# Performer attention of a 16-layer network: feature matmuls by row groups, head sums by column groups, one batch in two slots

## The chip, the cores and the metric

The kernel runs on one core of one Trainium2 chip, in one launch. The metric is the time of one execution in device microseconds. Before the change the median of three runs was 4373.4 us (4373.02 to 4376.56).

## The reference

The reference is a network of 16 layers on an array of 16 batches, 256 tokens and 128 channels. Each layer adds its result to x after a norm over the channels. The change touches one of them, the attention of `_L0_attn_b_ref` (a "performer"): 16 heads of 8 channels, 32 random features per head. Cut to that:

```python
def _phi(u, omega):                                  # u: b h s k (k=8), omega: m k (m=32)
    proj = jnp.einsum('bhsk,mk->bhsm', u, omega)
    sq = 0.5 * jnp.sum(u * u, axis=-1, keepdims=True)
    stab = jnp.max(proj, axis=-1, keepdims=True)
    return jnp.exp(proj - sq - stab) / jnp.sqrt(m) + 1e-06

q, k, v = (jnp.einsum('bsd,dhk->bhsk', x, w) for w in (wq, wk, wv))
pq, pk = _phi(q * scale, omega), _phi(k * scale, omega)
kv  = jnp.einsum('bhsm,bhsk->bhmk', pk, v)           # sums over the 256 tokens of a batch
z   = jnp.sum(pk, axis=2)
num = jnp.einsum('bhsm,bhmk->bhsk', pq, kv)
den = jnp.einsum('bhsm,bhm->bhs', pq, z)
out = (num / den[..., None]) ... @ wo
```

After it come a residual, a layer norm (`ln1`), a feed-forward part and a second layer norm.

## The kernel before

All activations stay on the chip as tiles of 128 channels (partitions) by 4096 tokens. Work goes by chunks of 512 tokens (8 of them, index `c`; a chunk is two batches), batches of 256 tokens (16, index `b`) and tiles of 128 tokens (32, index `n`). All matmuls are fp32.

`performer_attend` is written as steps. `tiles_in_slots` runs over slots `k` from -6 to 45 and in each slot goes down the list `steps`: an entry `(slot, every, many, what)` calls `what(n)` in slot `slot + n * every`. This is the program's order on every engine: each engine takes its instructions in this order, and a waiting one holds up those behind it. Four slots are one chunk. A PSUM bank is asked for with `self.bank()`; before the change all steps share eight banks, in turn.

The steps that matter, by name:

- `project(c)`: two matmuls (`wq`, `wk`) over a chunk; ScalarE copies each to `q` (scaled), GpSimd squares it to `sq`.
- `lengths(c)`: eight matmuls of `sq` against `w["half"]` give half the squared length of each head's vector; VectorE copies them to `nrm`. `values(c)`: four matmuls with `wv`, copied to `v` by ScalarE with a column of ones per group of four heads.
- `features(n)`: for one tile, the query side and the key side each take one matmul of 128 rows against the block-diagonal `w["om"]` (512 columns: 16 heads of 32 features). VectorE takes the maximum over each head's 32 features from PSUM (`tensor_reduce` into `sub`, L2298), adds `nrm`, and subtracts from PSUM into `f`; ScalarE takes the exponential of the 1024 columns, GpSimd scales and adds 1e-6 (L2304).
- `sums(b)`: eight matmuls (L504, 33 columns) of the key features against the values; VectorE masks them into `kv`. `turn(n)`: four transposes of the query features, copied to `ft` by ScalarE.
- `heads(n)`: four matmuls of `ft` against `kv` (36 columns: 32 sums and 4 denominators) give tokens by channels; VectorE takes the reciprocal of the denominators (L2340) and multiplies into `o`. `join(c)`: four transposes bring `o` back to channels by tokens, copied to `ot`.
- `out(c)`: one matmul with `wo`, and VectorE adds `h0` into `hb`. `end(0..2)`: the layer norm: a matmul that centres `hb`, a ScalarE copy, the square `nsq` on GpSimd, a matmul for the variance, Ln and Exp on ScalarE (`nrs`), a product on VectorE (L543) and a bias on ScalarE. `norm(0..2)`: the norm before the attention, for the last three chunks only; the other five were normed in the layer before.

The order within a slot before the change, from the list:

```python
(13, 4, NCH, end(2)), (12, 4, NCH, end(1)), (11, 4, NCH, end(0)), (10, 4, NCH, out), (9, 4, NCH, join),
(4, 1, NTILE, heads), (3, 2, B, sums), (2, 1, NTILE, turn), (0, 1, NTILE, features),
(-1, 4, NCH, lengths), (-1, 4, NCH, values), (-2, 4, NCH, project),
(-3, 4, NCH, norm(2)), (-5, 4, NCH, norm(1)), (-6, 4, NCH, norm(0)),
```

L504 is the helper `mm` (matmul), L508 `tr` (transpose), L528 `act` (ScalarE), L531 `tt` (VectorE), L534 `gt` (GpSimd). In the trace each fp32 matmul leaves two records.

Of the kernel before, what the change touches and what calls it, by code (L numbers as in the profile page):

```python
# [1649 lines left out]
class Fast(Net):  # L1650
# [598 lines left out]
    def performer_attend(self, w):  # L2249


        nc = self.nc
        h0, y = self.ha, self.hb
        s8 = 8.0**-0.25
        with ExitStack() as st:
            p = self.stage(st, "f2", 1)
            qk, nrm, vs, fs, kvs, fts, os, ots, ends = {}, {}, {}, {}, {}, {}, {}, {}, {}

            def project(c):
                s = self.chunk(c)  # L2260
                for side, wn in enumerate(("wq", "wk")):
                    pq = self.bank()
                    self.mm(pq, w[wn], h0[:, s])
                    q = p.tile([P, CH], F32, tag=f"q{side}", name="q", bufs=2)
                    self.act(q, pq, AF.Copy, scale=s8)
                    sq = p.tile([P, CH], F32, tag=f"sq{side}", name="sq", bufs=1)
                    self.gt(sq, q, q, ALU.mult)
                    qk[c, side] = q, sq

            def lengths(c):  # L2270
                pn = self.bank()
                for side in range(2):
                    for t in range(4):
                        at = (2 * t + side) * 16
                        self.mm(pn[:, at : at + 16], qk[c, side][1][:, t * P : t * P + P], w["half"])
                nrm[c] = p.tile([P, 4, 2, 16], F32, tag="nrm", name="nrm", bufs=2)
                nc.vector.tensor_copy(nrm[c].rearrange("p t s h -> p (t s h)"), pn[:, :P])
# [10 lines left out]
            def features(n):  # L2288
                c, t = divmod(n, 4)
                f = p.tile([P, 2, 16, 32], F32, tag="f", name="f", bufs=6)  # L2290
                sub = p.tile([P, 2, 16], F32, tag="sub", name="sub", bufs=2)
                pps = []
                for side in range(2):
                    pp = self.bank()
                    self.mm(pp, qk[c, side][0][:, t * P : t * P + P], w["om"])
                    pps.append(pp.rearrange("p (h m) -> p h m", h=16))
                for side in range(2):
                    nc.vector.tensor_reduce(sub[:, side], pps[side], AX.X, ALU.max)  # L2298
                self.tt(sub, sub, nrm[c][:, t], ALU.add)
                for side in range(2):  # L2300
                    self.tt(f[:, side], pps[side], sub[:, side, :, None].broadcast_to([P, 16, 32]), ALU.subtract)
                flat = f.rearrange("p s h m -> p (s h m)")
                self.act(flat, flat, AF.Exp)
                nc.gpsimd.tensor_scalar(flat, flat, 32.0**-0.5, 1e-6, ALU.mult, ALU.add)  # L2304
                fs[n] = f.rearrange("p s h m -> p s (h m)")

            def sums(b):
                pkv = self.bank()
                for g in range(4):
                    for u in range(2):  # L2310
                        n = 2 * b + u
                        self.mm(
                            pkv[:, g * 33 : g * 33 + 33], fs[n][:, 1, g * P : g * P + P], vs[n // 4][:, n % 4, g],
                            start=u == 0, stop=u == 1,
                        )
                kv = p.tile([P, 4, 36], F32, tag="kv", name="kv", bufs=2)
                pk3 = pkv[:, : 4 * 33].rearrange("p (g k) -> p g k", g=4)
                self.tt(kv[:, :, :32], pk3[:, :, :32], w["own"][:, None, :].broadcast_to([P, 4, 32]), ALU.mult)
                self.tt(
                    kv[:, :, 32:], pk3[:, :, 32:33].broadcast_to([P, 4, 4]),  # L2320
                    w["own1"][:, None, :].broadcast_to([P, 4, 4]), ALU.mult,
                )
                kvs[b] = kv

            def turn(n):
                pf = self.bank()
                for g in range(4):
                    self.tr(pf[:, g * P : g * P + P], fs[n][:, 0, g * P : g * P + P])
                ft = p.tile([P, 4, P], F32, tag="ft", name="ft", bufs=3)
                self.act(ft.rearrange("p g t -> p (g t)"), pf, AF.Copy)  # L2330
                fts[n] = ft

            def heads(n):
                ft, kv = fts.pop(n), kvs[n // 2]
                pn = self.bank()
                for g in range(4):
                    self.mm(pn[:, g * 36 : g * 36 + 36], ft[:, g], kv[:, g])
                pn3 = pn[:, :144].rearrange("p (g k) -> p g k", g=4)
                rd = p.tile([P, 4, 4], F32, tag="rd", name="rd", bufs=2)
                nc.vector.reciprocal(rd, pn3[:, :, 32:])  # L2340
                if n % 4 == 0:
                    os[n // 4] = p.tile([P, 4, P], F32, tag="o", name="o", bufs=2)
                self.tt(
                    os[n // 4][:, n % 4].rearrange("p (g h k) -> p g h k", g=4, h=4),
                    pn3[:, :, :32].rearrange("p g (h k) -> p g h k", h=4),
                    rd[:, :, :, None].broadcast_to([P, 4, 4, 8]), ALU.mult,
                )

            def join(c):
                pt = self.bank()  # L2350
                o = os.pop(c)
                for t in range(4):
                    self.tr(pt[:, t * P : t * P + P], o[:, t])
                ots[c] = p.tile([P, CH], F32, tag="ot", name="ot", bufs=1)
                self.act(ots[c], pt, AF.Copy)

            def out(c):
                s = self.chunk(c)
                ph = self.bank()
                self.mm(ph, w["wo"], ots.pop(c))  # L2360
                self.tt(y[:, s], h0[:, s], ph, ALU.add)

            def end(i):
                def step(c):
                    if i == 0:
                        s = y[:, self.chunk(c)]
                        ends[c] = self.norm_steps(p, s, s, "ps", w["ln1_g"], w["ln1_b"], "eps6")
                    ends[c][i]()

                return step  # L2370

            norm = lambda i: lambda c: self.norm_x_step(p, c, i)
            steps = [
                (13, 4, NCH, end(2)), (12, 4, NCH, end(1)), (11, 4, NCH, end(0)), (10, 4, NCH, out), (9, 4, NCH, join),
                (4, 1, NTILE, heads), (3, 2, B, sums), (2, 1, NTILE, turn), (0, 1, NTILE, features),
                (-1, 4, NCH, lengths), (-1, 4, NCH, values), (-2, 4, NCH, project),
                (-3, 4, NCH, norm(2)), (-5, 4, NCH, norm(1)), (-6, 4, NCH, norm(0)),
            ]
            self.tiles_in_slots(-6, NTILE + 14, steps)

    def performer_ffn(self, w):
        x, h0, y = self.x, self.ha, self.hb
# [1425 lines left out]
```

## Time and profile before

| | |
|---|---|
| median of the runs | 4373.4 us |
| profiled execution: time, span | 4392.96 us, 4391.2 us |
| share of the span busy: PE, PEld, VectorE, ScalarE, GpSimd | 90%, 50%, 59%, 54%, 48% |
| mean granted TensorE clock | 0.952 |
| attention stage, 870.3 to 1086.3 us | PE busy 205.15, VectorE 127.52, ScalarE 90.60, GpSimd 63.54 of 216.00; granted clock 0.94 |

The stage is about a twentieth of the span. It begins with the first matmul of `project` and ends with the last bias of the layer norm. Busy times are those of one profiled execution; PE's is the time in which matmuls are in the array, whatever the number of their columns.

### The profile page before, as it was taken

The page shows a single profiled execution, that of the slowest core. Times are in us where ns is not written, and L with a number is a line of the kernel's source. Part 1 is how long each engine was busy: PE and PEld are TensorE (multiplying, and loading weights), DVE is VectorE, ACT ScalarE, POOL GpSimd, SP SyncE. Part 2 cuts the span into 40 slices and gives each one's busy share as a digit, 9 for nine tenths or more (in the row PEclk, how much of TensorE's full clock was granted, in tenths as well). Part 3 has the DMA queues.
Part 4 walks back from the last instruction along what each step waited for, and adds up shares of the span by engine and source line. Part 5 has one row for each costly group of instructions (what it writes and reads, how often), then busy time and mean ns, then how long its engine had stood idle before and what let it go on. Part 6 is the DMA issues. An engine that isn't in the chain of part 4 may idle for free. (4 is left out here: it accounts for less than half of the span.)

```text
span 4391.2 us, 72802 instructions
## 1 busy us (share of the span) xinstructions
PE 3966.2 (90%) x28390; PEld 2202.4 (50%) x28390; DVE 2605.3 (59%) x4455; ACT 2376.1 (54%) x4549; POOL 2119.4 (48%) x1776
## 2 busy tenths in 40 slices
PE   7899999999899999995989969887999899899978
PEld 3455455466355445543975549643333344355333
DVE  4764566364366377456336643564888788386374
ACT  6665466444766456553447634445555554675442
POOL 4653355232455255315433334466998789521251
PEclk8999999999999999997999979998999999999989
DMA  1800000000000000001940029200000000000000
GB/s 59 332 1 1 11 1 1 19 1 1 19 1 1 1 3 1 1 0 49 310 162 10 15 88 326 86 18 16 1 1 1 3 1 1 15 2 18 6 0 20
DMA packets 78400, 176.36 MB, mean 40 GB/s; under 512 B 12606, under 2 KB 39108, under 8 KB 77920
## 3 DMA queue, kind: packets, MB, share of 16 engines
q1 hardware_dynamic: 65568, 148.40, 9.8%
q0 software_dynamic: 9120, 18.51, 1.2%
q8 instruction: 227, 3.72, 0.4%
q10 hardware_dynamic: 3360, 4.72, 0.3%
q14 instruction: 125, 1.02, 0.1%
HBM read 118.28 MB, written 54.20 MB: 39 GB/s over the span
## 5 line engine op out<-in xcount | busy, mean ns | idle before, releaser
L528 ACT ACTIVATE pt<-ps 128x512 f32<-128x512 f32 (+1 forms) x896 | 423.1, 537 | 408.1 <-PE ps L504 406.8
L504 PE MATMUL ps<-hb,w 128*128 128x512 f32 (+1 forms) x960 | 468.9, 623 | 5.4 <-issue 3.3
L531 DVE TENSOR_TENSOR t<-ps,tab 128x512 f32<-128x512 f32 x512 | 319.3, 683 | 196.1 <-ACT sq L528 191.3
L504 PE MATMUL ps<-w,hb 128*128 128x512 f32 (+2 forms) x896 | 415.1, 576 | 13.6 <-DVE t L531 11.3
L534 POOL TENSOR_TENSOR t<-t,ss 128x1024 f32<-128x1024 f32 x128 | 243.7, 1904 | 306.8 <-ACT ss L528 197.7
L534 POOL TENSOR_TENSOR t<-t,t 128x512 f32<-128x512 f32 x256 | 320.5, 1275 | 13.2 <-PE ps L504 10.1
L504 PEld LDWEIGHTS ps<-hb,w 128*128 128x128 f32 (+1 forms) x960 | 183.6, 196 | 273.5 <-issue 247.3
L531 DVE TENSOR_TENSOR u<-u,ps 128x384 f32<-128x384 f32 (+1 forms) x206 | 121.8, 595 | 277.8 <-ACT u L528 131.2
L534 POOL TENSOR_TENSOR nsq<-ha 128x512 f32<-128x512 f32 x112 | 123.2, 1100 | 314.1 <-ACT ha L528 297.3
L504 PE MATMUL ps<-nsq,ct 128*128 128x512 f32 x368 | 209.5, 654 | 53.9 <-POOL nsq L534 35.0
L528 ACT ACTIVATE pt<-pt 128x768 f32<-128x768 f32 (+1 forms) x160 | 169.5, 1060 | 154.6 <-DVE pt L531 154.6
L2199 POOL DMA_INDIRECT back<-y,x x142 | 139.1, 980 | 184.2 <-ACT y L528 90.2
L504 PE MATMUL ps<-qkt 64*128 64x192 f32 (+1 forms) x2048 | 216.2, 326 | 11.8 <-ACT pt L528 11.8
L504 PE MATMUL ps<-u,w 128*128 128x512 f32 (+1 forms) x448 | 218.8, 612 | 8.0 <-POOL u L534 8.0
L504 PE MATMUL ps<-ot,w 128*128 128x512 f32 x448 | 211.1, 604 | 15.2 <-POOL ot L534 6.9
L504 PE MATMUL ps<-xt,w 128*128 128x128 f32 x1704 | 219.8, 279 | 1.5 <-ACT xt L528 1.5
L504 PEld LDWEIGHTS ps<-qkt 64*128 64x128 f32 x2048 | 153.1, 188 | 133.3 <-ACT qkt L528 51.5
L504 PEld LDWEIGHTS ps<-w,hb 128*128 128x128 f32 x896 | 147.4, 192 | 139.4 <-issue 110.7
L531 DVE TENSOR_TENSOR pt<-ps,w 128x384 f32<-128x384 f32 (+1 forms) x320 | 171.2, 576 | 75.6 <-PE ps L504 72.2
L3705 POOL DMA_INDIRECT rows<-out,idx x128 | 126.4, 988 | 174.6 <-ACT out L528 125.6
L528 ACT ACTIVATE u<-ps,w 128x512 f32<-128x512 f32 x160 | 107.2, 685 | 186.3 <-PE ps L504 183.5
L531 DVE TENSOR_TENSOR pt<-pt,w 128x1024 f32<-128x1024 f32 (+1 forms) x96 | 181.1, 1886 | 42.3 <-ACT pt L528 42.3
(362 smaller groups left out, 9127.2 us busy)
## 6 DMA issues: line engine op xcount, KB each, us to landing
w<-in_moe_x SPq DMA_DIRECT2D x142, 533.0 KB
rows<-t SPq DMA_DIRECT2D x64, 520.0 KB
x<-rows SPq DMA_DIRECT2D x142, 65.0 KB
w<-in_local_f SPq DMA_DIRECT2D x8, 659.5 KB
y<-back ACTq DMA_DIRECT2D x16, 256.0 KB
y<-back SPq DMA_DIRECT2D x16, 256.0 KB
w<-in_local_f SPq DMA_DIRECT2D x4, 658.5 KB
back<-y,x POOLq DMA_INDIRECT x142
```

What stands on the lines that cost most here:

```text
L504: self.nc.tensor.matmul(out, lhsT, rhs, start=start, stop=stop)
L528: self.nc.scalar.activation(out, in_, func, **kw)
L531: self.nc.vector.tensor_tensor(out, a, b, op)
L534: self.nc.gpsimd.tensor_tensor(out, a, b, op)
L2199: nc.gpsimd.indirect_dma_start(views[i], bass.IndirectOffsetOnAxis(ap=x[:, C : C + 1].bitcast(I32), axis=0), y, None, bounds_check=2 * NT ...
L3705: nc.gpsimd.indirect_dma_start(views[(c * 2 + k) * 4 + t], bass.IndirectOffsetOnAxis(ap=idx[:, k, t : t + 1], axis=0), out[:, k, t], None,)
```

## The change

The change is confined to `performer_attend`.

- `features` works on a batch (two tiles, two sides) every second slot. Each of its 16 matmuls takes 32 rows (four heads) and 128 columns of `w["om"]`; the four row groups go to four PSUM banks. VectorE and ScalarE do the same work in two halves: two groups at a time are reduced, added, subtracted, exponentiated and scaled.
- PSUM is split: four banks (`f`) for `features`, four for all other steps.
- `kv` holds masked sums and masked denominators, 32 columns each. `heads` works on a batch: per group of four heads one matmul for the sums and one for the denominators, with `kv` as the 32 weight columns and `ft` as 256 moving columns, each group to its own 32 PSUM partitions. The result is channels by tokens. The division is Ln and Exp on ScalarE and a product on VectorE into `ot`.
- `join`, the reciprocal and `o` are gone. `lengths` writes in the order of the groups. The slots of `heads`, `sums` and `turn` move by one or two.

```diff
@@ lengths
+                by_group = pn[:, :P].rearrange("p (b g n h) -> p b g n h", b=2, g=4, h=4)
...
+                        self.mm(by_group[:, t // 2, :, t % 2 * 2 + side], qk[c, side][1][:, t * P : t * P + P], w["half"])
@@ features
-                f = p.tile([P, 2, 16, 32], F32, tag="f", name="f", bufs=6)
...
-                    self.mm(pp, qk[c, side][0][:, t * P : t * P + P], w["om"])
+                f = p.tile([P, 4, 2, 2, P], F32, tag="f", name="f", bufs=3)
+                sub = p.tile([P, 4, 16], F32, tag="sub", name="sub", bufs=2)
+                pps = [self.bank("f") for _ in range(4)]
+                for u in range(2):
+                    for side in range(2):
+                        for g in range(4):
+                            rows, t = slice(32 * g, 32 * g + 32), b % 2 * 2 + u
+                            self.mm(
+                                pps[g][:, (2 * u + side) * P : (2 * u + side) * P + P],
+                                qk[c, side][0][rows, t * P : t * P + P], w["om"][rows, g * P : g * P + P],
+                            )
+                for k in range(2):
+                    gs = slice(2 * k, 2 * k + 2)
+                    for g in (2 * k, 2 * k + 1):
+                        nc.vector.tensor_reduce(sub[:, g], pps[g].rearrange("p (n m) -> p n m", m=32), AX.X, ALU.max)
...
+                    self.act(flat, flat, AF.Exp)
+                    nc.gpsimd.tensor_scalar(flat, flat, 32.0**-0.5, 1e-6, ALU.mult, ALU.add)
@@ heads
+            def heads(b):
+                ft, kv = fts.pop(b), kvs.pop(b)
                 pn = self.bank()
-                for g in range(4):
-                    self.mm(pn[:, g * 36 : g * 36 + 36], ft[:, g], kv[:, g])
-                nc.vector.reciprocal(rd, pn3[:, :, 32:])
...
+                for k in range(2):
+                    for g in range(4):
+                        nc.tensor.matmul(pn[32 * g : 32 * g + 32, k * T : k * T + T], kv[:, k, g], ft[:, g], start=k == 0, stop=k == 1, skip_group_check=True)
+                rd = p.tile([P, T], F32, tag="rd", name="rd", bufs=2)
+                self.act(rd, pn[:, T:], AF.Ln)
+                self.act(rd, rd, AF.Exp, scale=-1.0)
...
+                self.tt(ots[b // 2][:, b % 2 * T : b % 2 * T + T], pn[:, :T], rd, ALU.mult)
-            def join(c):
...
@@ steps
-                (13, 4, NCH, end(2)), (12, 4, NCH, end(1)), (11, 4, NCH, end(0)), (10, 4, NCH, out), (9, 4, NCH, join),
-                (4, 1, NTILE, heads), (3, 2, B, sums), (2, 1, NTILE, turn), (0, 1, NTILE, features),
+                (13, 4, NCH, end(2)), (12, 4, NCH, end(1)), (11, 4, NCH, end(0)), (10, 4, NCH, out),
+                (6, 2, B, heads), (4, 2, B, sums), (3, 1, NTILE, turn), (0, 2, B, features),
                 (-1, 4, NCH, lengths), (-1, 4, NCH, values), (-2, 4, NCH, project),
...
-            self.tiles_in_slots(-6, NTILE + 14, steps)
+            with self.share(f=4, ps=4):
+                self.tiles_in_slots(-6, NTILE + 14, steps)
```

More of the change, by code (lines that the diff above doesn't have):

```diff
@@ L2256, in performer_attend @@
             p = self.stage(st, "f2", 1)
-            qk, nrm, vs, fs, kvs, fts, os, ots, ends = {}, {}, {}, {}, {}, {}, {}, {}, {}
+            qk, nrm, vs, fs, kvs, fts, ots, ends = {}, {}, {}, {}, {}, {}, {}, {}
             def project(c):
@@ L2271, in lengths @@
                 pn = self.bank()
+                by_group = pn[:, :P].rearrange("p (b g n h) -> p b g n h", b=2, g=4, h=4)
                 for side in range(2):
                     for t in range(4):
[L2274 to L2277, printed above, removed]
+                        self.mm(by_group[:, t // 2, :, t % 2 * 2 + side], qk[c, side][1][:, t * P : t * P + P], w["half"])
+                nrm[c] = p.tile([P, 2, 64], F32, tag="nrm", name="nrm", bufs=2)
+                nc.vector.tensor_copy(nrm[c].rearrange("p b n -> p (b n)"), pn[:, :P])
             def values(c):
@@ L2286, in values, with features @@
                 vs[c] = v
-            def features(n):
-                c, t = divmod(n, 4)
-                f = p.tile([P, 2, 16, 32], F32, tag="f", name="f", bufs=6)
[L2291 to L2294, printed above, removed]
-                    self.mm(pp, qk[c, side][0][:, t * P : t * P + P], w["om"])
[L2296 to L2305, printed above, removed]
+            def features(b):
+                c = b // 2
+                f = p.tile([P, 4, 2, 2, P], F32, tag="f", name="f", bufs=3)
[13 more added lines that the diff above has]
+                        nc.vector.tensor_reduce(sub[:, g], pps[g].rearrange("p (n m) -> p n m", m=32), AX.X, ALU.max)
+                    flat = sub[:, gs].rearrange("p g n -> p (g n)")
+                    self.tt(flat, flat, nrm[c][:, b % 2, 32 * k : 32 * k + 32], ALU.add)
+                    for g in (2 * k, 2 * k + 1):
+                        self.tt(
+                            f[:, g].rearrange("p u s (h m) -> p (u s h) m", h=4), pps[g].rearrange("p (n m) -> p n m", m=32),
+                            sub[:, g, :, None].broadcast_to([P, 16, 32]), ALU.subtract,
+                        )
+                    flat = f[:, gs].rearrange("p g u s m -> p (g u s m)")
+                    self.act(flat, flat, AF.Exp)
+                    nc.gpsimd.tensor_scalar(flat, flat, 32.0**-0.5, 1e-6, ALU.mult, ALU.add)
+                fs[b] = f
@@ L2310, in sums @@
                     for u in range(2):
-                        n = 2 * b + u
                         self.mm(
-                            pkv[:, g * 33 : g * 33 + 33], fs[n][:, 1, g * P : g * P + P], vs[n // 4][:, n % 4, g],
+                            pkv[:, g * 33 : g * 33 + 33], fs[b][:, g, u, 1], vs[b // 2][:, b % 2 * 2 + u, g],
                             start=u == 0, stop=u == 1,
                         )
-                kv = p.tile([P, 4, 36], F32, tag="kv", name="kv", bufs=2)
+                kv = p.tile([P, 2, 4, 32], F32, tag="kv", name="kv", bufs=2)
@@ L2317, in sums @@
                 pk3 = pkv[:, : 4 * 33].rearrange("p (g k) -> p g k", g=4)
[L2318 to L2322, printed above, removed]
+                own = w["own"][:, None, :].broadcast_to([P, 4, 32])
+                self.tt(kv[:, 0], pk3[:, :, :32], own, ALU.mult)
@@ L2323, in sums @@
+                self.tt(kv[:, 1], pk3[:, :, 32:33].broadcast_to([P, 4, 32]), own, ALU.mult)
                 kvs[b] = kv
             def turn(n):
+                b, u = divmod(n, 2)
+                if u == 0:
+                    fts[b] = p.tile([P, 4, T], F32, tag="ft", name="ft", bufs=2)
                 pf = self.bank()
                 for g in range(4):
-                    self.tr(pf[:, g * P : g * P + P], fs[n][:, 0, g * P : g * P + P])
-                ft = p.tile([P, 4, P], F32, tag="ft", name="ft", bufs=3)
@@ L2330, in turn @@
[L2330 to L2334, printed above, removed]
-                pn = self.bank()
-                for g in range(4):
-                    self.mm(pn[:, g * 36 : g * 36 + 36], ft[:, g], kv[:, g])
-                pn3 = pn[:, :144].rearrange("p (g k) -> p g k", g=4)
-                rd = p.tile([P, 4, 4], F32, tag="rd", name="rd", bufs=2)
-                nc.vector.reciprocal(rd, pn3[:, :, 32:])
[L2341 to L2347, printed above, removed]
@@ L2349, in join @@
-            def join(c):
[L2350 to L2355, printed above, removed]
+                    self.tr(pf[:, g * P : g * P + P], fs[b][:, g, u, 0])
+                self.act(fts[b][:, :, u * P : u * P + P], pf.rearrange("p (g t) -> p g t", g=4), AF.Copy)
+            def heads(b):
+                ft, kv = fts.pop(b), kvs.pop(b)
+                pn = self.bank()
+                for k in range(2):
[4 more added lines that the diff above has]
+                self.act(rd, rd, AF.Exp, scale=-1.0)
+                if b % 2 == 0:
+                    ots[b // 2] = p.tile([P, CH], F32, tag="ot", name="ot", bufs=2)
+                self.tt(ots[b // 2][:, b % 2 * T : b % 2 * T + T], pn[:, :T], rd, ALU.mult)
```

## The prediction

> **What bounds the kernel now.** The stage's busy times by stretches come first. The starts of the chunks' first feature matmuls (899.0, 919.2, 942.2, 966.9, 991.6, 1016.3, 1039.3 in the timeline) give the period: 24.7 us for a chunk in which the three norm steps also run, 23.0 without them, 20.2 at the start. Columns: length, then busy time (and instructions) of PE, PEld, DVE, ACT, POOL, granted clock, DMA.
>
> ```profile
> 966.90:991.60 24.70, 24.70 (x140) 17.48 (x139) 16.09 (x36) 12.12 (x20) 8.35 (x9) 1.00 0.00 1
> ...
> 1073.10:1076.60 3.50, 1.12 (x2) 0.30 (x2) 0.75 (x1) 1.41 (x3) 0.00 (x0) 0.99 0.00 0
> 1076.60:1080.00 3.40, 2.07 (x2) 0.50 (x2) 0.69 (x1) 0.54 (x1) 0.00 (x0) 0.50 0.00 0
> 1080.00:1083.40 3.40, 2.17 (x3) 1.14 (x4) 0.00 (x0) 0.12 (x2) 1.04 (x1) 0.50 0.00 0
> ```
>
> In a period TensorE has matmuls in the array all the time at clock 1.00; VectorE is 65% busy. TensorE bounds the stage. The last rows, the stage's end, show something else: where TensorE waits a large part of 3.4 us, the granted clock is 0.50 in the next stretch.
>
> The groups by shape, for 880 to 1080 us (last columns: busy, mean ns, idle before and what ended it):
>
> ```profile
> L504 PE MATMUL ps<-w,q 128*128 128x512 f32 x127 | 60.9, 604 | 0.0
> L504 PE MATMUL ps<-kv,ft 128*128 128x36 f32 x256 | 32.9, 276 | 0.0
> L504 PE MATMUL ps<-v,f 128*128 128x33 f32 x256 | 31.3, 277 | 0.6 <-POOL f L2304 0.6
> L528 ACT ACTIVATE f<-f 128x1024 f32<-128x1024 f32 x32 | 33.8, 1057 | 95.7 <-DVE f L531 95.7
> ```
>
> Records of 512 columns start 0.43 us apart, narrow ones about 0.1075, so a chunk takes: features 16 x 0.43 = 6.9, heads 32 x 0.1075 = 3.4, sums 3.4, turn 1.7, lengths 1.7, values 0.9, join 0.4, project 1.7, out 0.9, end 1.7, norm 1.7. The sum is 24.4 of the 24.7 measured.
>
> Last the timeline, for how long one link takes to hand over to the next. Columns: start, length.
>
> ```profile
> 980.81 1.06 ACT L528 ACTIVATE f<-f 128x1024 f32<-128x1024 f32 x1 [2.89 <-DVE f L531]
> 981.77 1.07 ACT L528 ACTIVATE q<-ps 128x512 f32<-128x512 f32 x2
> 981.95 1.05 POOL L2304 TENSOR_SCALAR f<-f 128x1024 f32<-128x1024 f32 x1 [3.38 <-ACT f L528]
> 983.07 2.04 POOL L534 TENSOR_TENSOR sq<-q 128x512 f32<-128x512 f32 x2
> 985.92 1.85 PE L504 MATMUL ps<-w,sq 128*128 128x16 f32 x16
> ...
> 1049.67 1.31 DVE L2298 TENSOR_REDUCE sub<-ps 128x16 f32<-128x512 f32 x2
> 1051.01 0.19 DVE L531 TENSOR_TENSOR sub<-sub,nrm 128x32 f32<-128x32 f32 x1
> 1051.24 1.29 DVE L531 TENSOR_TENSOR f<-ps,sub 128x512 f32<-128x512 f32 x2
> ```
>
> The first five lines are a chain: exponential, then the copies of q, which stand behind it on ScalarE, then the squares, which stand behind the scaling of f on GpSimd, then lengths. Today TensorE has other work meanwhile.
>
> **What TensorE saves.** Row and column groups run side by side elsewhere in this trace:
>
> ```profile
> 2513.92 1.14 PE L504 MATMUL ps<-qz,k 32*128 32x512 f32 x8
> 2514.99 0.66 PE L508 MATMUL ps<-ct,ha 128*128 128x128 f32 x4
> ...
> 3212.44 1.93 PE L3259 MATMUL ps<-pt,v 128*32 128x256 f32 x32
> 3214.19 0.61 PE L3259 MATMUL ps<-both,ct 128*32 128x256 f32 x8
> ```
>
> Eight records on four row groups take 1.07 us where eight in a row take 3.4; 32 records of 256 columns on four column groups take 1.75 us. So features(b), 32 records of 128 columns on four row groups, takes 8 x 0.1075 + 0.1 = 0.98 us, and heads(b), 16 records of 256 columns on four column groups, 0.98 us. Per chunk: minus 6.9, 3.4 and 0.4 (join), plus 4 x 0.98: TensorE's work falls from 24.4 to 17.6 us.
>
> **What the new order makes of it.** Per chunk VectorE's sum changes little: 16.1 us, minus four reciprocals (0.25) and four o products (0.29), plus two ot products (0.42 each, between the 0.29 of 128 columns and the 0.68 of 512; a 128x256 row has 0.424) and 2 x 0.13 for the wider denominators (128 columns at 0.29 for 16 at 0.16): 15.1. ScalarE's gets two Ln (0.39) and Exp (0.42), loses the ot copy (0.58): 13.2. No engine has 24 us of work, so if the stage keeps its length a chain does it. I follow the chains from the order of the instructions of the changed kernel, which the slot list fixes. Features now hold all four f banks until VectorE's last subtraction, so two batches of features never overlap.
>
> Chain A, from the first batch of a chunk to the second. VectorE's run for a batch: two times 2.86 us (1049.67 to 1052.53) = 5.7. Behind its last subtraction ScalarE has, in this order: the second exponential (0.1 until it starts, 0.96 until the next), the bias of end(2) (0.62 from start to start), the copy of turn (0.48), and only then Ln and Exp of heads (0.42, 0.42, from rows of another stage, 152.64 to 153.48). Then VectorE takes 0.1, ot 0.42, two kv products 0.58, and the next reductions. Sum: 9.8 us. TensorE needs 4.0 for turn, out, heads and sums; the second turn takes the bank that out's addition frees, which stands on VectorE behind the run, the L543 product and sometimes a norm product: about 7.5. So TensorE waits some 3.5 us, and its features are done at about 9.1, before ot.
>
> Chain B, from the second batch to the next chunk's first. Run 5.7, handover 0.1, second exponential 1.06, handover 0.1, scaling of f on GpSimd 1.05, two squares 2.04, handover 0.1: 10.2 us until lengths can finish, because project stands behind features in its slot and its q copies behind both exponentials. TensorE has project, norm(0), end(0) and a turn until then, 3.9 us, and then waits about 5.4. Behind it in TensorE's queue: the key half of lengths 0.86, values 0.86, norm(1) 0.86, end(1) 0.86, heads 0.98, sums 1.72, turn 0.43, features 0.98, and 0.2 until VectorE starts. Sum: 17.9.
>
> A + B = 27.7 us against 24.7 in the three chunks with norms, and 26.8 against 23.0 without. Over eight chunks: 3 x 3.0 + 5 x 3.8 = +28 us, with the clock at 1.00. I count the head and the tail as chunks.
>
> **The clock.** Before, it held 1.00 from 900 to 1060 us. Now each chunk has TensorE waits of about 3.5 and 5.4 us, longer than those that cost it the clock at the stage's end. The shortest half-clock stretch there is 3.4 us; in it TensorE does 1.7 us of work. On chain B 7.6 us of TensorE work follows the wait and all of it is on the path: one stretch costs 1.7 us, two cost 3.4. In chain A turn and features follow, 1.4 us with 0.7 of slack: up to 0.7. The bounds are 0 and 4.1 us a chunk, 0 and 33 us in all; I take 2.5 a chunk, +20, one stretch in B and the slack used up in A, as the nearest rows, the stage's end, show the loss in nearly every wait. The Trainium skill ("TensorE: Matmul & The Clock Gate", section "Why this matters for your kernels") says to leave no idle gap over about 3 us between bursts, since one idle window of about 3.4 us halves the clock. It speaks against this change; by it both waits lose the clock, and the sum has the upper bound.
>
> The same skill ("TensorEngine Tiling (Array Packing)", section "PSUM Bottleneck") warns that after tiling the copies out of PSUM may bound. By that alone the chunk would come to VectorE's 15 to 16 us, a gain; what I price is VectorE's and ScalarE's order, not their sums.
>
> **The sum.** +28 and +20 give +48 us: the profiled 4392.96 would become 4441, the median 4373.4 (19.5 lower, a difference I carry over) 4421. I say 4420. A change under 0.2%, about 9 us, can't be told from none.
>
> **The rivals.**
> 1. *TensorE's work decides, faster.* If the waits were covered as they are now, 6.8 us fewer a chunk would give 8 x -6.8 = -54: 4319. For it: PE 24.70 of 24.70. Against: it needs A + B under 24.7 (23.0), 3 to 4 us less than the order allows, and features have no second set of banks. It would come about if squares and copies did not stand behind the batch's exponentials. 7%, partial gains included.
> 2. *The chains, with the clock kept.* +28: 4401. For it: the matmuls that remain are dense, and the attention ran 160 us at 1.00. Against: waits of over 3 us each period. 28%.
> 3. *The row groups don't run side by side* (their weight loads of 128 columns in a queue). Features take 3.4 us a batch: +2.4 in B, +1.8 in A, 8 x 4.2 = +34 on top of +48: 4455. Against: the qz rows, though with 512 columns per load. 5%.
> 4. *No measurable change*, the chains shorter by 3 us a chunk: 4373. 4%.
>
> The forecast has 56%. The range: 4388 (half the loss of the second rival, for chains that overlap at handovers) to 4446 (both clock bounds, +61, and 12 for head, tail and the switches between full array and groups, which no row prices singly). Faster by over 0.2% is rival 1, 7%; within 0.2% rival 4, 4%; slower the rest, 89%.
>
> **What would show it.** Right: TensorE busy in the stage under 80%, a period of 27 to 32 us, each chunk with a wait of lengths (ps<-w,sq) on GpSimd of 4 us or more and one of a turn on VectorE; ot on VectorE waiting for ScalarE's rd; granted clock in the stage well under 0.94; features as 32*128 records in four at a time. Wrong: a period under 23 us; lengths without a wait; or the clock at 1.00 throughout, which leaves the second rival.

## The result: 1.56% slower, and the profile after

The changed kernel takes 4440.7 us (median of 4 runs, 4438.2 to 4443.2) against 4373.2 of the kernel before (4367.3 to 4376.6): ratio 1.0156, 95% interval 1.0138 to 1.0173. The profiled execution took 4440.45 us, its span is 4438.7.

**Where the time went.** The `qkt` matmuls of the local layers serve as a landmark: the last of them lie well behind the stage. The first fence is the row of that tile before the change, the second after it (min/median/max ns, then first and last start in us).

```profile
L504 PE MATMUL ps<-qkt x2048: 272/322/687, 140.9 to 1841.0; 64*128 64x192 f32 x94, 64*128 64x128 f32 x93
```

```profile
L504 PE MATMUL ps<-qkt x2048: 272/322/686, 140.7 to 1908.5; 64*128 64x192 f32 x94, 64*128 64x128 f32 x93
```

Up to there the changed kernel lost 67.5 us, which is the whole difference of the medians (67.5). Nearly all of it is in the stage: from the last `ps<-u,w` matmul before the stage to the first `qkt` matmul behind its feed-forward part, before took 329.0 us and after 392.9, so +63.9. Behind 1841.0 and 1908.5 the order is the other way round: 4391.2 - 1841.0 = 2550.2 us before, 4438.7 - 1908.5 = 2530.2 after. That is why the spans differ by 47.5 us only.

**The periods.** The first feature matmuls of the chunks start at 878.45, 907.36, 938.01, 967.18, 998.61, 1031.38, 1063.40 and 1095.26: periods of 28.9, 30.7, 29.2, 31.4, 32.8, 32.0 and 31.9 us, against 20.5, 20.2, 23.0, 24.7, 24.7, 24.7 and 23.0. The busy times by stretches of the profile after: one whole chunk, then four stretches of it of the length at which the clock changed. Columns: length, then busy time (and instructions) of PE, PEld, DVE, ACT, POOL, granted clock, DMA.

```profile
967.18:998.61 31.43, 25.08 (x184) 17.54 (x183) 14.17 (x30) 13.34 (x22) 8.37 (x9) 0.78 0.00 1
```

```profile
970.60:974.01 3.41, 2.11 (x20) 1.86 (x16) 3.34 (x8) 1.06 (x1) 1.09 (x1) 0.94 0.00 0
974.01:977.42 3.41, 2.08 (x24) 1.76 (x27) 1.73 (x5) 3.33 (x6) 1.05 (x1) 0.50 0.02 5
...
984.25:987.66 3.41, 0.83 (x5) 0.63 (x6) 0.00 (x0) 3.34 (x6) 2.34 (x3) 0.94 0.01 2
987.66:991.08 3.42, 3.42 (x17) 3.42 (x18) 0.00 (x0) 0.00 (x0) 2.80 (x4) 0.50 0.00 0
```

TensorE is busy 25.08 of 31.43 us, although its work at full clock is 17.6 by the prediction's sum. Each of the two stretches with a TensorE wait is followed by one at clock 0.50. No other engine is near its limit: VectorE 14.17, ScalarE 13.34. The groups by shape, 938 to 1063 us, show the half clock in the means and the idle time with its releasers:

```profile
L504 PE MATMUL ps<-v,f 128*128 128x33 f32 x128 | 15.8, 278 | 0.0
L504 PE MATMUL ps<-w,sq 128*128 128x16 f32 x64 | 14.4, 375 | 8.1 <-POOL sq L534 8.1
L504 PE MATMUL ps<-w,q 32*128 32x128 f32 x257 | 13.3, 356 | 0.0
L508 PE MATMUL ps<-ct,f 128*128 128x128 f32 x65 | 11.5, 302 | 19.3 <-DVE hb L531 10.9 <-ACT q L528 8.4
```

The sums (`ps<-v,f`) run at 278 ns as before (277); the lengths (`ps<-w,sq`) went from 259 in the groups of before to 375. The turns (`ps<-ct,f`) wait 19.3 us, in four chunks, for VectorE's addition `hb` and ScalarE's copies `q`.

The timeline of the chunk holds both ways through the engines (start, length):

```profile
968.37 1.29 DVE L2305 TENSOR_REDUCE sub<-ps 128x16 f32<-128x512 f32 x2 [1.06 <-PE ps L504]
...
975.34 1.12 PE L508 MATMUL ps<-ct,f 128*128 128x128 f32 x4 [2.63 <-DVE hb L531]
...
976.38 2.09 PE L504 MATMUL ps<-w,q 32*128 32x128 f32 x32
...
976.96 0.42 DVE L531 TENSOR_TENSOR ot<-ps,rd 128x256 f32<-128x256 f32 x1 [1.68 <-ACT rd L528]
...
978.49 1.29 DVE L2305 TENSOR_REDUCE sub<-ps 128x16 f32<-128x512 f32 x2 [0.71 <-PE ps L504]
...
985.79 0.63 PE L508 MATMUL ps<-ct,f 128*128 128x128 f32 x4 [2.69 <-ACT q L528]
...
986.37 2.04 POOL L534 TENSOR_TENSOR sq<-q 128x512 f32<-128x512 f32 x2
...
987.46 3.59 PE L504 MATMUL ps<-w,sq 128*128 128x16 f32 x16 [1.04 <-POOL sq L534]
...
990.89 2.06 PE L504 MATMUL ps<-w,ha 128*128 128x128 f32 x8
...
999.80 1.29 DVE L2305 TENSOR_REDUCE sub<-ps 128x16 f32<-128x512 f32 x2 [1.06 <-PE ps L504]
```

From reductions to reductions, chain A takes 968.37 to 978.49 = 10.1 us and chain B 978.49 to 999.80 = 21.3 us, together the period of 31.4. The lengths, 1.85 us before, take 3.59 at half clock; so do the features of the second batch with 2.09 instead of 1.17.

### The profile page after: what moved, and what is told of

The parts are those of the page before. It is cut to its first block, busy times and chain, and to the rows that moved or that the text cites. A ratio compares the mean times of both kernels' runs of the same rounds, so it can differ in the third digit from the quotient of the medians.

```text
span 4438.7 us, 73417 instructions
## 1 busy us (share of the span) xinstructions
PE 3967.5 (89%) x28742; PEld 2202.1 (50%) x28742; DVE 2599.4 (59%) x4407; ACT 2381.9 (54%) x4573; POOL 2116.6 (48%) x1776
## 5 line engine op out<-in xcount | busy, mean ns | idle before, releaser
L534 POOL TENSOR_TENSOR t<-t,t 128x512 f32<-128x512 f32 x256 | 320.2, 1273 | 13.0 <-PE ps L504 10.1
L531 DVE TENSOR_TENSOR u<-u,ps 128x384 f32<-128x384 f32 (+1 forms) x206 | 121.7, 595 | 287.2 <-PE ps L508 184.0
L528 ACT ACTIVATE pt<-pt 128x768 f32<-128x768 f32 (+1 forms) x160 | 169.6, 1060 | 155.0 <-DVE pt L531 155.0
L531 DVE TENSOR_TENSOR ot<-ps,rd 128x512 f32<-128x512 f32 (+2 forms) x224 | 142.4, 636 | 179.8 <-ACT rd L528 179.8
L528 ACT ACTIVATE nrs<-ps,ct 128x512 f32<-128x512 f32 x208 | 140.1, 685 | 127.9 <-PE ps L504 122.7
```

The lines of the kernel that those rows point to most:

```text
L528: self.nc.scalar.activation(out, in_, func, **kw)
L531: self.nc.vector.tensor_tensor(out, a, b, op)
L534: self.nc.gpsimd.tensor_tensor(out, a, b, op)
```

## Experiments: which part of the change costs

The theory to be tested: the batch of features turns a stage that TensorE's work bounded into one that two ordered chains bound, and TensorE's waits in them cost it the clock. The rivals: row groups that do not run side by side or hinder one another; the split of the banks; the column groups with Ln and Exp; the clock alone. Ratios are to the kernel before on the same chip (4372 to 4396 us, by chip). "Stage" is the time between the landmarks above in the one profiled execution (329.0 before). "Clock" is the granted clock from 960 to 1060 us (1.00 before; 0.78 in the first profile of the changed kernel). Two profiles of the changed kernel itself have 392.9 and 396.6 us for the stage, so a difference of 4 us in that column says nothing.

| run | ratio (95% interval) | stage, us | clock |
|---|---|---|---|
| changed kernel again | 1.0155 (1.0139 to 1.0170) | 396.6 | 0.76 |
| column groups alone | 0.9980 (0.9971 to 0.9989) | 321.3 | 0.99 |
| the same, output earlier | 0.9980 (0.9971 to 0.9989) | 317.4 | 1.00 |
| split of the banks alone | 1.0030 (1.0019 to 1.0041) | 339.5 | 0.95 |
| row groups by tile, shared banks | 1.0018 (1.0009 to 1.0027) | 341.8 | 0.84 |
| the same with full rows | 0.9998 (0.9989 to 1.0007) | 329.7 | 1.00 |
| row groups by tile, split banks | 1.0041 (1.0027 to 1.0055) | 345.6 | 0.79 |
| changed, full rows | 1.0212 (1.0198 to 1.0226) | 422.3 | 0.85 |
| changed, projections early | 1.0121 (1.0105 to 1.0136) | 384.4 | 0.77 |
| changed, TensorE kept busy | 1.0134 (1.0117 to 1.0151) | 389.9 | 0.90 |
| changed, both of these | 1.0117 (1.0101 to 1.0134) | 381.1 | 0.86 |
| changed, projections early and features first | 1.0080 (1.0064 to 1.0095) | 362.6 | 0.81 |

**The changed kernel again.** 

> The changed kernel as it is, beside the others on one chip, since the kernel before takes 4394.3 on the chip of the last four runs and 4373.2 on the first. If the loss is the stage's own, the ratio to the kernel before is again 1.0156 within 0.002.

Measured 1.0155, on a chip on which before takes 4395.8 us. The ratio is the same on this second chip.

**Column groups alone.** The kernel before with `heads` of the changed kernel; `join`, the reciprocal and `o` go.

```diff
-(13, 4, NCH, end(2)), ..., (10, 4, NCH, out), (9, 4, NCH, join),
-(4, 1, NTILE, heads), (3, 2, B, sums),
+(13, 4, NCH, end(2)), ..., (10, 4, NCH, out),
+(5, 2, B, heads), (3, 2, B, sums),
```

> The kernel before with one part of the change alone: the column groups. The heads are done for a batch of two tiles by 16 matmuls that write their sums by channels, with the reciprocal by Ln and Exp on ScalarE, and the join with its four transposes is gone; the features stay by tile with 128 rows, all eight banks stay shared, and heads stand at slot 5 of a batch. Theory (TensorE bounds the kernel before, and only the batches of features turn the order into the bound): a chunk loses 16 matmuls of 36 columns (16 x 0.215 = 3.4 us) and four transposes (0.43) and gains two times 0.98 us, so 1.9 us a chunk at most, in seven chunks 13; about 8 of it reach the end: 4360 to 4368, against 4373.2. Rival (the column groups with Ln and Exp on ScalarE are what makes the change slow): most of the 67 us appear here: 4400 or more.

Measured 0.9980, or 9 us faster. From 960 to 1060 us:

```profile
960.00:1060.00 100.00, 94.22 (x556) 57.48 (x556) 61.80 (x125) 53.21 (x89) 31.77 (x35) 0.99 0.00 1
```

TensorE stays busy with its clock kept, and the saved work reaches the end. This half of the change is a gain; it beats both kernels.

**The same, with output and end two slots earlier.**

```diff
-(13, 4, NCH, end(2)), (12, 4, NCH, end(1)), (11, 4, NCH, end(0)), (10, 4, NCH, out),
+(11, 4, NCH, end(2)), (10, 4, NCH, end(1)), (9, 4, NCH, end(0)), (8, 4, NCH, out),
```

> The kernel with the column groups alone (features by tile, eight shared banks), with the projection to the output and the three steps of the second normalisation two slots earlier (8 to 11 in place of 10 to 13), since the sums by channels are there right after the heads of a chunk's second batch and no join follows. Theory: TensorE's work per chunk stays, but the stage ends two slots (two quarters of a chunk's 23 us, less what other work has to follow anyway) earlier: 3 to 7 us under the run with the column groups alone, ratio 0.9965 to 0.9975. Rival (the output's projection now waits on ScalarE's logarithm and exponential and stops TensorE behind it): as fast as that run or slower, 0.998 to 1.002, with a wait of the matmuls from ot on VectorE ot.

The ratio is the same 0.9980. The stage is 3.9 us shorter in its profile, which is no more than two profiles of one kernel differ by, and the timed runs show nothing of it. The wait that the rival named is there, and small. The waits of its trace (total, times, longest):

```profile
PE ps L504 <- DVE ot L531: 3.6, 2, 3.2
```

So the theory's 3 to 7 us did not come; this wait is one cost that the trace shows, and whether it took all of them stays open.

**Split of the banks alone.** The kernel before, with four banks for the features of a tile and four for all else.

```diff
-                    pp = self.bank()
+                    pp = self.bank("f")
...
-            self.tiles_in_slots(-6, NTILE + 14, steps)
+            with self.share(f=4, ps=4):
+                self.tiles_in_slots(-6, NTILE + 14, steps)
```

> The kernel before with one part of the change alone: its banks are split, four for the features of a tile (two sides, so two tiles' worth) and four for all else, in place of eight shared by all. Theory (the split costs something by itself, but the loss is the batch that holds all four banks until VectorE has read them): 5 to 12 us, ratio 1.001 to 1.003, and part of the row-groups-by-tile run's 18 us is this. Rival (the split costs nothing): within 3 us, ratio 0.9993 to 1.0007. Rival (four banks for all else are the bottleneck of the changed kernel): 30 us or more, 1.007 and up.

Measured 1.0030, 13 us, at the theory's upper end. The split is a cost of its own, but a fifth of the loss.

**Row groups by tile, split banks.** Both kinds of groups, no batches of features: a tile's 8 matmuls go to four half-used banks.

```diff
+                pps = [self.bank("f") for _ in range(4)]
+                for side in range(2):
+                    for g in range(4):
+                        rows = slice(32 * g, 32 * g + 32)
+                        self.mm(pps[g][:, side * P : side * P + P], qk[c, side][0][rows, ...], w["om"][rows, ...])
```

> The kernel before with both parts of the change but without the batches of features: row groups of four heads each for one tile at a time, in four banks that are half used, with all VectorE work, exponential and scaling by tile as before and the same split of the banks into four and four; heads by batch. VectorE's reductions and subtractions are eight of 256 elements a tile instead of four of 512. Theory (the batch in two slots makes the loss, not the row groups): a first result is there after half the VectorE run and the period stays near 24.5 us: 4365 to 4385. Rival (row groups do not run side by side, or four banks for features and four for all else are too few): 4405 or more, with features' records at over 1 us a tile.

Measured 1.0041, 18 us: above the theory's 4365 to 4385, far below the rival. A tile's features take 0.73 us at full clock, so the groups do run side by side. What differs from here to the changed kernel is the batch, with the slots of `sums`, `turn` and `heads` and the sizes of VectorE's and ScalarE's instructions that go with it: 1.0155 - 1.0041 = 1.14%, or 50 of the 67 us.

**Row groups by tile, shared banks.** The same without the split.

```diff
-                pps = [self.bank("f") for _ in range(4)]
+                pps = [self.bank("ps") for _ in range(4)]
```

> The kernel with row groups by tile and heads by batch, but with all eight banks shared as before (the split into four and four undone). Theory (the split and the batch are what costs; row and column groups themselves do not): the 18 us over the kernel before go by the 13 that the split alone costs and a little more, since TensorE's saved work is not bound by the banks any more: ratio 0.998 to 1.002. Rival (row groups or the eight smaller VectorE instructions a tile cost by themselves): 1.003 to 1.006.

Measured 1.0018, at the upper end of the theory. But it is 0.38% slower than the column groups alone, with less TensorE work; the next run asks why. Three successive stretches of this kernel:

```profile
988.41:991.83 3.42, 3.42 (x32) 1.97 (x30) 0.36 (x1) 2.54 (x6) 3.34 (x4) 1.00 0.03 5
991.83:995.24 3.41, 3.41 (x41) 3.12 (x41) 2.16 (x8) 0.60 (x1) 1.51 (x2) 0.98 0.00 0
995.24:998.65 3.41, 3.41 (x12) 2.78 (x13) 1.61 (x5) 1.54 (x2) 0.73 (x1) 0.52 0.00 0
```

In the first two TensorE has matmuls in the array without a gap, and in the third its clock still drops to 0.52.

**The same with full rows.** Row groups undone, all else kept: the same matmuls take 128 rows.

```diff
-                        rows = slice(32 * g, 32 * g + 32)
-                        self.mm(pps[g][...], qk[c, side][0][rows, t * P : t * P + P], w["om"][rows, g * P : g * P + P])
+                        self.mm(pps[g][...], qk[c, side][0][:, t * P : t * P + P], w["om"][:, g * P : g * P + P])
```

> The run with row groups by tile, heads by batch and eight shared banks, with the row groups alone undone: the same 8 matmuls of features a tile take all 128 rows, into the same columns of the same four half-used banks. TensorE's features grow from 0.73 to about 1.7 us a tile, 4 us a chunk. That run had a granted clock of 0.84 from 960 to 1060 us with no wait of TensorE over 1.3 us, and is 0.4% slower than the one with the column groups alone. Theory A (the four half-used banks of a tile and VectorE's eight smaller instructions cost that): the same or up to 8 us more than with row groups: ratio to the kernel before 1.0015 to 1.0040. Theory B (the row groups' short matmuls themselves lose the clock, and that is what costs): the clock is back above 0.95 and the time is that of the column groups alone: 0.997 to 0.9995. Between the two, 0.9995 to 1.0015: each has a part.

Measured 0.9998, in the field between the theories. The stretch from 960 to 1060 us, first with row groups, then with full rows:

```profile
960.00:1060.00 100.00, 90.89 (x708) 61.18 (x706) 56.92 (x168) 49.10 (x82) 31.28 (x34) 0.84 0.00 1
```

```profile
960.00:1060.00 100.00, 95.52 (x750) 76.31 (x750) 63.93 (x190) 50.84 (x87) 33.38 (x36) 1.00 0.00 1
```

The features grow from 0.73 to 1.95 us a tile, the clock goes from 0.84 to 1.00 and the kernel gets 0.20% faster. So about half of the 0.38% goes with the row groups, although they are the shorter matmuls; what the two stretches show against them is the clock. The two ratios come from two chips, and their intervals only just part. The other half stays with what this run keeps, the four half-used banks and VectorE's smaller instructions, which no run separates.

**Changed, full rows.** The same edit in the changed kernel, where features come by batch.

> The changed kernel with the row groups alone undone: each of the same matmuls of features takes all 128 rows of the queries' channels and of the block diagonal weights, into the same columns of the same four banks; batches, banks, VectorE's work and order are as changed. Theory (the ordered way decides, and the features' matmuls lie in it once a batch): 16 x 0.215 = 3.44 us a batch instead of 0.98 to 1.17 where the clock is full, 2.3 to 2.5 more in two batches of a chunk, less what longer matmuls keep of the clock: 25 to 40 us over the changed kernel, ratio to the kernel before 1.021 to 1.025. Rival (the row groups do not run side by side, or their writes hinder one another, and are the loss): as fast as the changed kernel or faster, 1.016 or less. Rival (TensorE does not lie on the way, VectorE alone does): 1.0145 to 1.0170.

Measured 1.0212: 25 us more than the changed kernel, at the theory's lower end. In the timeline the features of a batch are 3.74 us at full clock and 4.84 partly at half clock:

```profile
991.54 4.84 PE L504 MATMUL ps<-w,q 128*128 128x128 f32 x32
```

Here the row groups are a gain, as the features lie on both chains. The rival of groups that hinder one another falls.

**Changed, projections early.**

```diff
-                (-1, 4, NCH, lengths), (-1, 4, NCH, values), (-2, 4, NCH, project),
-                (-3, 4, NCH, norm(2)), (-5, 4, NCH, norm(1)), (-6, 4, NCH, norm(0)),
+                (-1, 4, NCH, lengths), (-1, 4, NCH, values),
+                (-3, 4, NCH, norm(2)), (-3, 4, NCH, project), (-5, 4, NCH, norm(1)), (-6, 4, NCH, norm(0)),
```

> The changed kernel with one step moved: the projections of a chunk go from slot -2 to slot -3, behind the last step of its normalisation, so that their copies and squares on ScalarE and GpSimd no longer stand behind the exponentials of the batch whose slot they shared. Theory (the ordered way through the engines): the way from a chunk's second batch to the next chunk's first (22.2 us after the change) loses the exponential of the second batch, the scaling and the two squares, and TensorE's lengths no longer wait for GpSimd there; the period of a chunk falls by 1.5 to 2.5 us in seven chunks, so 10 to 18 us of 4440.7: about 4427. Rival (the row groups themselves or the split of the banks into four and four cost the time): the same instructions in the same banks, so no change within 4 us: 4437 to 4445. Rival (TensorE's half clock alone): the records of lengths and values stay at half clock and the time falls by less than 5 us.

Measured 1.0121, 15 us less: the theory's range, and neither rival's. It gives no more because a new wait comes in the chunks with norms, where the projections now follow the norm's product `ha`, which stands on VectorE behind a whole batch (waits of TensorE, 960 to 1060 us):

```profile
PE ps L504 <- DVE ha L531: 12.8, 2, 6.4
```

**Changed, TensorE kept busy.** Useless matmuls are added, and overwritten.

```diff
             def lengths(c):
                 pn = self.bank()
+                if c:
+                    for _ in range(4):
+                        self.mm(pn, w["wq"], h0[:, self.chunk(c)])
```

> The changed kernel with useless work added: in each chunk but the first, four matmuls of 512 columns (0.86 us each at full clock) write the bank of the lengths before these overwrite it; they need only normalised inputs that are long there, so TensorE does them in its wait for the squares of GpSimd, and the output is unchanged. They add 3.4 us of TensorE work a chunk, 24 us in all. Theory (half clock after a wait is a large part of the loss): the lengths that follow take 1.7 to 2.0 us instead of 3.59, the values 1.1 instead of 2.06, and the time is no longer, or falls by up to 12 us: 4429 to 4440. Rival (the order of the steps alone; the clock costs nothing because TensorE waits anyway): the lengths' records get shorter but the time grows by the part of the added work that no wait covers, 5 to 15 us: 4446 to 4456.

Measured 1.0134, 9 us less with 24 us more work, though the two intervals overlap, so the time shows no more than that the added work costs nothing. The timeline has lengths and values at full clock:

```profile
992.03 1.85 PE L504 MATMUL ps<-w,sq 128*128 128x16 f32 x16
...
993.73 1.14 PE L504 MATMUL ps<-w,ha 128*128 128x128 f32 x8
```

The granted clock rises from 0.76 to 0.90. The rival that the half clock costs nothing (4446 to 4456 against 4373, so 1.0166 and up) falls. That the half clock lies on the path is seen in the next chunk. First the changed kernel, then this run; the rows are the features of the second batch, the lengths, and the next chunk's first features:

```profile
1007.93 2.09 PE L504 MATMUL ps<-w,q 32*128 32x128 f32 x32
...
1019.01 3.59 PE L504 MATMUL ps<-w,sq 128*128 128x16 f32 x16 [1.04 <-POOL sq L534]
...
1031.38 1.17 PE L504 MATMUL ps<-w,q 32*128 32x128 f32 x32
```

```profile
1009.63 2.09 PE L504 MATMUL ps<-w,q 32*128 32x128 f32 x32
...
1022.97 1.85 PE L504 MATMUL ps<-w,sq 128*128 128x16 f32 x16
...
1030.84 1.17 PE L504 MATMUL ps<-w,q 32*128 32x128 f32 x32
```

With the added matmuls the lengths start 13.3 us behind the features instead of 11.1, and the next chunk's features still come after 21.2 us instead of 23.5. The chunk after that is alike (21.2 against 22.3). In the chunk before, where the added matmuls ran partly at half clock (5.12 us), there is no gain: 22.9 against 22.2.

**Changed, both edits.**

> Both edits of the earlier runs: the projections early and the four useless matmuls of 512 columns a chunk ahead of the lengths (output unchanged). Theory (order and clock are two losses): the two gains add up in part, since with the squares early less of the added 3.4 us is covered: ratio 1.0100 to 1.0120. Rival (the wait for the squares and the half clock behind it are one loss, and the one edit takes all of it): the added work shows in full or in part, 1.0125 to 1.016.

Measured 1.0117, in the theory's range, but against 1.0121 of the projections early alone this is no difference. The two single edits have medians of 4451.3 and 4451.5 us on one chip. How far the two gains overlap is not settled.

**Changed, projections early and features first.** `(0, 2, B, features)` moves to the head of the list.

> The run with the projections early, and besides the features of a batch placed ahead of the other steps of their slot (ends, output, heads, sums, turn) instead of behind them. Theory (the ordered way): the way from a chunk's second batch to the next chunk's first loses heads, sums and a turn as well (1.07 + 1.97 + 0.54 in the profile of the changed kernel), of which other work that VectorE must still do takes part back: 5 to 10 us less than with the projections early, ratio to the kernel before 1.009 to 1.011. Rival (the features' banks, read by VectorE, set the time of a batch whatever stands ahead): as the run with the projections early, 1.011 to 1.0135.

Measured 1.0080, 18 us less than with the projections early alone and better than the theory's 1.009 to 1.011. Half of the loss goes by a change of order, with TensorE's work unchanged; the clock, at 0.81, is little better than the 0.76 to 0.78 of the changed kernel.

**The account.** Four kernels differ by one part each, from column groups alone to the whole change: 0.9980, then row groups by tile 1.0018, then the split 1.0041, then the batch 1.0155. In us of 4373: -9, +17, +10, +50, the first to 4 us, the others to between 6 and 9; together 68. How the 50 of the batch divide between the order of the steps, the clock and the banks that a batch holds, no run separates; the order alone gives back 33 of the 68. The banks seldom hold TensorE up by themselves: its waits for VectorE to free them are 2.41 and 1.38 us in the changed kernel's first chunk and 0.31 in its second, and none in the later ones, where a turn waits ahead of the features.

## Why the prediction was right in its case and short in its size

The case that was forecast came: slower, by ordered chains and a lost clock. 4440.7 lies in the range of 4388 to 4446, near its upper end, 20 us above the 4420 that was named.

**What TensorE saves: right.** Features of a batch take 1.17 us at full clock and heads 1.07, where 0.98 was forecast for each. (The prediction's own 8 x 0.1075 + 0.1 is 0.96, which changes nothing.) All four rivals fall: the saving did not decide (1), the clock was not kept, 0.78 in the chunk shown (2), the row groups run side by side (3), and the change is far above what can be told from none (4).

**Chain A: right.** 10.1 us against 9.8 in the chunk shown. The turn does wait for the bank that out's addition frees, for 2.63 us where 3.5 was forecast, and `ot` waits for ScalarE's `rd`.

**Chain B: right up to the lengths, short behind them.** From the reductions to the end of the squares 978.49 to 988.41 = 9.9 us (10.2). From there 11.4 us to the next reductions, against 7.7: what is left of the lengths 2.48 instead of 0.86, values 1.85 instead of 0.86, norm and end 2.49 instead of 1.72, the rest 4.57 instead of 4.3. The 3.4 us of the first three are two stretches at half clock, which the prediction had as its bound; it took one stretch, 1.7. The form of the wait differed in part. A wait of the lengths on GpSimd of 4 us or more was named for each chunk, and four of the seven passages from chunk to chunk have it (5.40, 5.38, 4.95 and 5.13 us). In the three with norms a turn waits first, 2.62 to 3.10 us, for ScalarE's copies of `q`, and the lengths then 1.04 us.

From reductions to reductions over all seven periods, chain A adds up to 66.9 us (7 x 9.8 = 68.6) and chain B to 149.0 (3 x 17.9 and 4 x 17.0 = 121.7). So what the chains lack in sum lies in B, 3.9 us a chunk, where the prediction set 1.7 for the clock. A is short in the first three chunks (7.4 to 9.5) and takes 10.1 to 10.7 in the later ones; in the chunk shown its reductions wait 0.71 us for features at half clock.

**The sum: three terms too small.** Chains of 27.7 and 26.8 us would have made the seven periods 3 x 27.7 + 4 x 26.8 = 190.3; they are 216.8. So the clock, with what else the chains lack, cost 26.5 where 7 x 2.5 = 17.5 was set: 9.0 short. The first two periods before were 20.5 and 20.2, and the prediction had read them, but worked with 23.0: 5.3 short. The seven periods thus lost 56.0. What is left of the 63.9 is 7.9, against 6.3 set for an eighth chunk: 1.6 short. Of the 7.9, 6.9 lie between the last chunk's first features and the feed-forward part, 0.2 ahead of the first chunk and 0.8 in the feed-forward part. That makes 15.9, the whole of 63.9 - 48. The last 3.6 us of the 67.5 came outside (3.9 in the layer that follows, less 0.3 ahead of the stage) and were not in the sum.

**The 19.5 us: wrong.** The profiled execution of before lay 19.5 us above the median, and the prediction carried that over. The changed kernel's profiled execution, 4440.45, is its median. The difference belongs to the part behind the last `qkt` matmul: 2550.2 us in the profiled execution of before. On chips where before takes 4394 to 4396 us that part took 2547.6 to 2555.5 in the profiles of this study, on those with 4372 to 4375 only 2523.7 to 2531.3, whatever the kernel. A profile from a chip of the first kind beside a median from one of the second would explain the 19.5 us; which chip the profile came from is not known, nor why the chips differ there. The agreement of the profiled time (4440.45) with the 4441 that the prediction named for it is chance: a stage 16 us longer than forecast met an end part 20 us shorter.

**The clock and the rule on it.** The Trainium skill ("TensorE: Matmul & The Clock Gate", section "Why this matters for your kernels") asks for no idle gap over about 3 us. The prediction set 2.5 us a chunk where that rule gave 4.1; 26.5 over seven chunks, 3.8 each, is nearer to the rule. The 2.5 rests in part on a misreading: "The shortest half-clock stretch there is 3.4 us". At the stage's end before the change the clock stays at 0.50 for three such stretches in a row, from 1062.9 to 1073.1 and again from 1076.6 to 1086.8. The prediction shows two of the latter, and this is the third, with TensorE busy throughout:

```profile
1083.40:1086.80 3.40, 3.40 (x5) 1.33 (x5) 0.75 (x1) 2.46 (x4) 0.00 (x0) 0.50 0.00 0
```

The trace is stricter than the rule. Behind the waits of 2.63 and of 2.69 us in this chunk the clock is at half too, and the row groups by tile lost it with no wait over 1.3 us. Nor is the length of one wait the measure: the 0.94 of the stretch 970.60:974.01, if the clock goes from 1.00 to 0.50 at once, puts the drop about 0.4 us before its end, when the wait that ends at 975.34 had lasted only some 0.9 of its 2.63 us.

## What to carry to other kernels

Before work on the bounding engine is made shorter, the order of its queue has to be followed for one whole period: what is bound by an engine's sum today may be bound by a chain through three engines tomorrow, above all if a larger unit of work makes another engine's run longer, as VectorE's 5.7 us for a batch, behind which the next steps then stand. Try the halves of such a change singly: here one half gains 0.2% and the rest costs some 1.8%. And the offset between a profile and a median goes into a forecast only where both are known to come from the same chip.

## What the hardware showed unexpectedly

TensorE's clock fell without waits. With row groups of 32 rows by tile, TensorE was busy 3.41 of 3.41 us in two successive stretches at 1.00 and 0.98, most of them heads, sums of 33 columns, transposes, row groups and lengths of 16 columns, and had 0.52 in the next; 128 rows for the same matmuls brought 100 us at 1.00, and the longer matmuls made the kernel 0.2% faster. In this case, then, the busy time of the profile does not tell whether the clock holds. What the gate counts, these runs do not show; that it counts how much of the array works is my reading only.
